# Two attention layers on one core: the transfers that fold the softmax sums, put in another order in two DMA queues

## The chip, the cores and the metric

The kernel runs on one core of a Trainium2 chip. The metric is the device time of one execution in microseconds (us); the median of three runs of the kernel before is 2529.92 us (2529.29 to 2533.68).

The names of a profile are used throughout: PE is the matrix engine (PEld its weight loads), DVE the vector engine, ACT the scalar engine, POOL and SP the two engines that issue the DMA transfers here. POOL's transfers can add to what lies at the destination; SP's only copy.

## The reference

Sixteen images of 256 channels and 32 x 32 positions go through two layers. Each layer normalises its input by groups and adds an attention over the 1024 positions, with 4 heads of 64 channels:

```python
q, k, v = proj(Wq, bq), proj(Wk, bk), proj(Wv, bv)     # of the group-normalised x
sim = jnp.einsum('bhdi,bhdj->bhij', q, k)
qpos = jnp.einsum('hdi,bhdj->bhij', rel, q)            # rel = rel_h + rel_w
attn = jax.nn.softmax(sim + qpos, axis=-1)
out = jnp.einsum('bhdn,bhmn->bhdm', v, attn)
x = x + out                                            # once for each layer
```

All is float32. What matters below is the denominator of the softmax: for every head and position a sum of 1024 exponentials.

## The kernel before, in words

**Units, pairs, blocks.** A unit is one image in one layer (32 of them; images of both layers are interleaved). A unit has two pairs of heads (`pr` 0 and 1), and a pair is worked in two halves of 512 positions. So a unit is four blocks, `n` counts blocks, and `b` is 0 to 3 in a unit. Blocks 0 and 2 of a unit are even ones (the pair's first half), 1 and 3 are odd. `block(n)` writes out by hand, for one block, what every engine is to do and in what order; the program runs in that order on each engine.

**A block's main work.** For each of 8 slices `j`, DVE writes the position term into PSUM (`seed`, L503), PE adds the scores (L539), ACT takes the exponential (L552) into a tile `p`, and PE multiplies the eight `p` with the values (`attend`, L592). ACT moves the result out of PSUM with `take_out` (the COPY of line L653, one for each block). Between these, PE, ACT and DVE do the projections and norms of the next unit.

**The sums.** The eight `p` of a block are added to a denominator in these steps:

- `add_up(blk, 1)`: DVE makes a tile `first` of `p` 0 and 1 (L557), and a POOL transfer adds `p` 2 to it (L568).
- `add_up(blk, 4)` and on: DVE makes a tile `acc` of `p` 3 and 4 (L557) and adds `p` 5, 6 and 7 (L572), the last one in the next block.
- `add_first` (POOL, L609) adds `first` to `acc`: 128 rows.
- `fold` (POOL, L614) adds `acc`'s upper 64 rows to its lower 64.
- `stack_up` (SP, L628, two transfers) copies rows 0 to 31 of each head into a tile `stack`, and `fold_again` (POOL, L633, two transfers) adds rows 32 to 63 there. With that, `acc` has been read for the last time. `stack` holds both halves of a pair.
- `fold_stack` (POOL, L638), five steps, folds the 128 rows of `stack` to 64, 32, 16, 8 and 4; `R` is 32 and `D` is 64, so the steps are `D`, `R`, `R // 2`, `R // 4`, `R // 8`.
- `spread_sums` (SP, L646, four transfers) writes the four rows to `den_all`; DVE takes reciprocals (L688), SP sends them through DRAM (L690, L695), and `finish` (DVE, L703 and L710) normalises and adds the residual. A finished image goes out by L712; the next image comes in by L113.

**Buffers.** `first` and `acc` share a pool of four buffers under one tag, handed out in turn:

```python
apool = ctx.enter_context(tc.tile_pool(name="apool", bufs=4))
```

A block takes two of them, so `acc` of block `n` takes the buffer of `acc` of block `n - 2`, and DVE's L557 waits until both `fold_again` transfers of block `n - 2` have landed. In the same way `first` of block `n` waits for `add_first` of block `n - 2`. There are two `stack` tiles.

**What sets the order.** Each engine works through its own instructions in the program's order. A transfer that waits for another one's landing holds up everything behind it in its queue. In the program before, `fold`, `stack_up` and `fold_again` of an even block stand together in the odd block after it; `stacked` and `summed` are the pairs whose `stack` is folded in odd and even blocks.

Of the kernel before, what the change touches and what calls it, by code (L numbers as in the profile page):

```python
# [56 lines left out]
def fast_path(ctx, tc, sh, x, layers, out, W, den_all, good, flag):  # L57
# [27 lines left out]
    B, C, H, N, CC, NT, NH, D, GT = (  # L85
        sh.B, sh.C, sh.H, sh.N, sh.CC, sh.NT, sh.NH, sh.D, sh.GT
    )
# [86 lines left out]
    def psum2(tag, name):  # L174
        i = 2 * "abcd".index(tag)
        return banks[:, i : i + 2, :]
# [252 lines left out]
    def values(u, g, pv, first=None):  # L429
        l = units[u][1]  # L430
        vts[u, g] = vpool.tile([P, NT // 2, C], F32, tag="v", name=f"v_{u}_{g}")
        pv = pv.rearrange("p a (b c) -> p a b c", c=C)

        def part(t, i, cc, rs, a):
            for x, c in enumerate(QUARTERS):
                j0 = (4 * g + 2 * a + i) * P + x * D
                yield nc.tensor.matmul(  # L437
                    pv[c, a, i, :],
                    xns[u][rs, cc, j0 : j0 + D],
                    W.wv[l][rs, cc, :],  # L440
                    start=(t == 0 and cc == 0 and i == 0),
                    stop=(t == 1 and cc == CC - 1 and i == 1),
                    skip_group_check=True,
                )

        def products(t):
            rounds = [
                [part(t, i, cc, rs, a) for rs, a in BANKS[t]]
                for i in range(2)
                for cc in range(CC)  # L450
            ]
            if t == 0 and first is not None:
                yield from woven(rounds, first)
            else:
                for r in rounds:
                    for p in r:
                        yield from p

        def out_of_psum():
            v = vts[u, g].rearrange("p (a b) c -> p a b c", a=2)  # L460
            for a in range(2):
                nc.scalar.copy(v[:, a], pv[:, a])  # L462

        return stretches(products), out_of_psum
# [62 lines left out]
    def scores(blk, j, tag=None, halves=False):  # L527

        u, pr, half = blk
        ps = psum2(tag, f"ps_{u}_{pr}_{half}_{j}") if tag else seeds.pop((blk, j))  # L530
        columns = slice(half * HALF, (half + 1) * HALF)
        for x, c in enumerate(QUARTERS):
            for h, hs in enumerate(QUARTERS):
                j0 = j * P + x * D
                terms = [(ks[u, pr], qs[u, pr])]
                if tag:
                    terms = [(qs[u, pr], wide[u, pr])] + terms
                for i, (a, b) in enumerate(terms):
                    nc.tensor.matmul(  # L539
                        ps[c, h, :],  # L540
                        a[hs, j0 : j0 + D],
                        b[hs, columns],
                        start=bool(tag) and i == 0,
                        stop=i == len(terms) - 1,
                        skip_group_check=True,
                    )
        p = ppool.tile([P, 2, HALF], F32, tag="p", name=f"p_{u}_{pr}_{half}_{j}")
        if halves:
            for h in range(2):
                nc.scalar.activation(p[:, h, :], ps[:, h, :], AF.Exp, bias=W.shift)  # L550
        else:
            nc.scalar.activation(p, ps, AF.Exp, bias=W.shift)  # L552
        probs[blk, j] = p

    def new_sum(blk, name, a, b):
        t = apool.tile([P, 2, HALF], F32, tag="acc", name=f"{name}_{blk[0]}_{blk[1]}_{blk[2]}")
        nc.vector.tensor_tensor(t, probs[blk, a], probs[blk, b], ALU.add)  # L557
        return t

    def add_up(blk, j):  # L560
        if index[blk] >= FOLDED:
            if j == 1:
                accs[blk] = new_sum(blk, "acc", 0, 1)
            elif j > 1:
                nc.vector.tensor_tensor(accs[blk], accs[blk], probs[blk, j], ALU.add)  # L565
        elif j == 1:
            firsts[blk] = new_sum(blk, "first", 0, 1)
            nc.gpsimd.dma_start(firsts[blk], probs[blk, 2], accum_op=ALU.add)  # L568
        elif j == 4:
            accs[blk] = new_sum(blk, "acc", 3, 4)  # L570
        elif j > 4:
            nc.vector.tensor_tensor(accs[blk], accs[blk], probs[blk, j], ALU.add)  # L572
# [32 lines left out]
    R = P // 4  # L605
    stacks = {}

    def add_first(blk):
        nc.gpsimd.dma_start(accs[blk], firsts.pop(blk), accum_op=ALU.add)  # L609

    def fold(blk):

        acc = accs[blk]
        nc.gpsimd.dma_start(acc[:D], acc[D:], accum_op=ALU.add)  # L614

    def beside(blk):

        u, pr, x = blk
        for h in range(2):
            yield h, stacks[u, pr][2 * x + h : P : 4, :]  # L620

    def stack_up(blk):

        u, pr, x = blk
        if x == 0:
            stacks[u, pr] = spool.tile([P, HALF], F32, tag="stack", name=f"stack_{u}_{pr}")
        for h, at in beside(blk):
            nc.sync.dma_start(at, accs[blk][:R, h, :])  # L628

    def fold_again(blk):  # L630
        acc = accs.pop(blk)
        for h, at in beside(blk):
            nc.gpsimd.dma_start(at, acc[R:D, h, :], accum_op=ALU.add)  # L633

    def fold_stack(u, pr, rows_):

        stack = stacks[u, pr]
        nc.gpsimd.dma_start(stack[:rows_], stack[rows_ : 2 * rows_], accum_op=ALU.add)  # L638

    def spread_sums(u, pr):  # L640

        stack, n = stacks.pop((u, pr)), index[u, pr, 0]
        for x in range(2):
            for h, hs in enumerate(QUARTERS):
                g = 2 * x + h
                nc.sync.dma_start(den_all[hs, n + x, :], stack[g : g + 1, :])  # L646
# [77 lines left out]
    def finish(u, pr):  # L724
        normalise(u, pr)
        add_residual(u, pr)
# [28 lines left out]
    blocks = [(u, pr, half) for u in range(NU) for pr in range(CC) for half in range(NH)]  # L755
# [32 lines left out]
    def block(n):  # L788
# [4 lines left out]
        last = n == len(blocks) - 3  # L793
# [5 lines left out]
        stacked = blocks[n - 3][:2] if not even and n > 2 else None  # L799
        summed = blocks[n - 4][:2] if even and n > 3 else None  # L800
        before = blocks[n - 6][:2] if even and n > 5 else blocks[n - 5][:2] if last else None
        after, previous = blocks[n + 1], blocks[n - 1] if n > 0 else None
        two = u + 2 < NU
        folded = previous and n - 1 < FOLDED
# [5 lines left out]
            add_up(previous, 7)  # L810
        if folded and even:
            add_first(previous)
        if even:
            qk = psum2(tz, f"qk_{w}_{pr}") if not plain else None
            first = None if plain else first_product(w, pr, qk)
            v, v_out = values(w, 1 - b // 2, psum2(tx, f"pv_{w}_{b}"), first)
# [11 lines left out]
                after_first(w, pr, qk)  # L828
            scores(blk, 2)
            add_up(blk, 1)  # L830
            if summed:
                fold_stack(*summed, R // 8)
                spread_sums(*summed)
            v(1)
            if folded:
                fold(previous)
            v_out()
            scores(blk, 3)
            seed(blk, 4, tb)
# [58 lines left out]
            scores(after, 1)  # L898
            seed(after, 2, ta)
            add_up(blk, 6)  # L900
            if summed and n == FOLDED:
                reciprocals(*summed)
            seed(after, 3, tb)
            norms(u, b, 4)
# [3 lines left out]
        else:  # L908
# [8 lines left out]
            if n == 1:  # L917
                reduced(2, 1)
                added(2)
            if stacked:  # L920
                fold_stack(*stacked, D)
            if stacked:
                fold_stack(*stacked, R)
            if not plain:
                k_half(w, pr, 1, qk)
            norms(u, b, 0)
# [11 lines left out]
            norms(u, b, 1)  # L938
            seed(blk, 7, tx)
            add_up(previous, 7)  # L940
            if folded:
                add_first(previous)
            if n > 4 and not last:
# [19 lines left out]
            if two:  # L963
                mean_out = (norm_mean if b == 1 else norm_var)(u + 2, pm)
            scores(after, 0)
            if folded:
                fold(previous)
                stack_up(previous)
            if stacked:
                fold_stack(*stacked, R // 2)  # L970
            if folded:
                fold_again(previous)
            if u + 3 < NU and units[u + 3][1] == 0 and u > 0 or n == 3:
                load_x(units[u + 3][0], range(pr_, pr_ + 1) if u > 0 else range(CC))
            seed(after, 1, tx)
            if last:
                finish(*before)
            if stacked:
                fold_stack(*stacked, R // 4)
                if last:  # L980
                    fold_stack(*stacked, R // 8)
                    spread_sums(*stacked)
            if two:
                mean_out()
                if b == 3:
# [17 lines left out]
    FOLDED = len(blocks) - BPU  # L1003
# [118 lines left out]
    def added(u):  # L1122
        part = parts.pop(u)
        reds[u] = small.tile([P, G], F32, tag="red", name=f"red_{u}")
        nc.vector.tensor_tensor(reds[u], part[:, 0, :], part[:, 1, :], ALU.add)
# [83 lines left out]
    v, v_out = values(0, 0, psum2("d", "pv_0_0"))  # L1209
# [7 lines left out]
    for n in range(len(blocks)):  # L1217
        if n in (1, 2):
            forms(n - 1)
        block(n)  # L1220
# [290 lines left out]
```

## Time and profile before

| what | value |
| --- | --- |
| median of three runs | 2529.92 us |
| the profiled execution | 2537.24 us, of it span 2535.5 us |
| granted clock of PE, mean | 0.995 |
| busy share of the span: PE, DVE, ACT, POOL | 98%, 93%, 81%, 31% |
| transfers from POOL: first<-p, acc<-first, acc<-acc, stack<-acc, median to landing | 8.0, 5.6, 4.5, 2.8 us |
| idle time of POOL before its `stack<-acc` transfers (L633) | 842.2 us |
| idle time of DVE before it makes `acc` (L557) | 32.0 us |

The span is the time from the first to the last instruction of the program in the profiled execution. Busy shares are averages over the span, and matmuls overlap each other, so that a PE of 98% can still lose time in places. A wait is listed with what ended it; "issue" there means that the profile shows nothing that ended it.

### The profile page before, as it was taken

The numbers are of one execution on the slowest core, as the hardware profiler recorded it, in microseconds if no ns is written. First come the engines' busy times: TensorE is split into PE (matmuls) and PEld (weight loads), VectorE is DVE, ScalarE is ACT, GpSimd is POOL, SyncE is SP. The second block draws the span as 40 slices with busy tenths as digits, with TensorE's granted clock in tenths as the row PEclk, the third lists the DMA queues.
The fourth block names the chain that finished last, engine by engine and source line by source line (L and its number), as shares of the span: only waits on it lengthen the run. The fifth ranks groups of instructions, "written<-read, shape, count | busy, mean of one in ns | idle before, by whom it ended". The sixth has DMA issues, their size and how long they took to land. (4 is left out here: it accounts for less than half of the span.)

```text
span 2535.5 us, 86433 instructions
## 1 busy us (share of the span) xinstructions
PE 2482.9 (98%) x36976; PEld 1766.0 (70%) x36976; DVE 2362.9 (93%) x2816; ACT 2057.3 (81%) x4296; POOL 796.4 (31%) x937
## 2 busy tenths in 40 slices
PE   7999999999999999999999999999999999999997
PEld 4777777777767767777676777767776676677764
DVE  7899999999999999899999999999999999899998
ACT  5888888888888888788887888888878888788764
POOL 0223333333333333333332333333333333333230
PEclk9999999999999999999999999999999999999999
DMA  2555556566556555665565556565665555556552
GB/s 86 111 96 104 109 111 112 110 129 137 111 109 141 112 105 111 124 120 113 116 115 118 114 111 121 108 132 115 120 126 119 114 104 112 109 95 122 113 112 73
DMA packets 137704, 286.64 MB, mean 113 GB/s; under 512 B 55896, under 2 KB 57432, under 8 KB 137312
## 3 DMA queue, kind: packets, MB, share of 16 engines
q0 software_dynamic: 71568, 195.12, 44.6%
q1 hardware_dynamic: 65744, 85.90, 11.9%
q8 instruction: 293, 4.80, 0.8%
q14 instruction: 99, 0.81, 0.1%
HBM read 51.78 MB, written 17.30 MB: 27 GB/s over the span
## 5 line engine op out<-in xcount | busy, mean ns | idle before, releaser
L503 DVE TENSOR_TENSOR banks<-abt 128x1024 f32<-128x1024 f32 x1207 | 1239.6, 1060 | 100.5 <-ACT p L552 58.6
L552 ACT ACTIVATE p<-banks,shift 128x1024 f32<-128x1024 f32 x898 | 980.1, 1114 | 278.1 <-PE banks L539 162.4
L539 PE MATMUL banks<-q,k 64*64 64x512 f32 x8192 | 1114.5, 593 | 9.6 <-DVE banks L503 9.6
L592 PE MATMUL banks<-p,v 64*64 64x256 f32 x16384 | 963.6, 377 | 0.0
L592 PEld LDWEIGHTS banks<-p,v 64*64 64x64 f32 x16384 | 783.1, 133 | 182.6 <-issue 38.9
L539 PEld LDWEIGHTS banks<-q,k 64*64 64x64 f32 x8192 | 470.9, 133 | 305.6 <-issue 121.4
L633 POOL DMA_DIRECT2D stack<-acc x248 | 210.8, 964 | 842.2 <-DMA stack<-acc 688.1
L572 DVE TENSOR_TENSOR acc<-acc,p 128x1024 f32<-128x1024 f32 x372 | 454.0, 1220 | 4.2
L638 POOL DMA_DIRECT2D stack<-stack x310 | 309.9, 1000 | 386.4 <-DMA stack<-stack 225.1
L401 PE MATMUL banks<-t,form 64*64 64x512 f32 x1984 | 405.2, 589 | 0.0
L437 PE MATMUL banks<-Wv,xn 64*64 64x256 f32 x4096 | 302.1, 378 | 0.7 <-ACT v L462 0.7
L437 PEld LDWEIGHTS banks<-Wv,xn 64*64 64x64 f32 x4096 | 229.8, 133 | 43.6 <-PEq L193 17.5
L401 PE MATMUL banks<-xn,form 64*64 64x512 f32 x992 | 259.3, 589 | 0.0
L288 ACT ACTIVATE xn<-x,nshift,rstd 128x128 f32<-128x128 f32 x496 | 211.7, 500 | 29.4 <-DVE nshift L281 29.4
L568 POOL DMA_DIRECT2D first<-p x124 | 220.6, 1779 | 36.7 <-ACT p L552 33.3
L614 POOL DMA_DIRECT2D acc<-acc x124 | 103.1, 831 | 386.0 <-DMA acc<-first 373.4
L213 ACT ACTIVATE junk<-x,neg 128x128 f32<-128x128 f32 x505 | 199.9, 404 | 0.0
L609 POOL DMA_DIRECT2D acc<-first x124 | 185.5, 1496 | 36.6 <-DVE acc L572 33.3
L401 PEld LDWEIGHTS banks<-t,form 64*64 64x64 f32 x1984 | 137.7, 133 | 71.1 <-issue 33.9
L557 DVE TENSOR_TENSOR acc<-p,p 128x1024 f32<-128x1024 f32 x128 | 156.2, 1221 | 32.0 <-issue 18.2
L550 ACT ACTIVATE p<-banks,shift 128x512 f32<-128x512 f32 x252 | 159.5, 684 | 23.1 <-PE banks L539 17.3
L557 DVE TENSOR_TENSOR first<-p,p 128x1024 f32<-128x1024 f32 x124 | 150.9, 1217 | 2.4 <-DMA acc<-first 2.1
(102 smaller groups left out, 1761.9 us busy)
## 6 DMA issues: line engine op xcount, KB each, us to landing
first<-p POOLq DMA_DIRECT2D x124, 512.0 KB, 8.0
acc<-first POOLq DMA_DIRECT2D x124, 512.0 KB, 5.6
rden<-rd SPq DMA_DIRECT2D x126, 256.0 KB, 4.4
acc<-acc POOLq DMA_DIRECT2D x124, 256.0 KB, 4.5
x<-in_x_dram SPq DMA_DIRECT2D x32, 512.0 KB, 3.8
stack<-acc SPq DMA_DIRECT2D x248, 64.0 KB, 2.1
stack<-acc POOLq DMA_DIRECT2D x248, 64.0 KB, 2.8
out_dram<-x SPq DMA_DIRECT2D x31, 512.0 KB, 2.9
```

Source lines behind the costliest of these rows:

```text
L288: nc.scalar.activation(grouped(xns[u], g), grouped(xt[units[u][0]], g), AF.Identity, bias=shift[:, g : g + 1], scale=rstd[:, g : g + 1],)
L401: yield nc.tensor.matmul(ps[c, a, :], f[rs, left[a], c0 : c0 + D], right[a][rs, :], start=(t == 0 and step == 1 and a == 1), stop=(t == 1) ...
L437: yield nc.tensor.matmul(pv[c, a, i, :], xns[u][rs, cc, j0 : j0 + D], W.wv[l][rs, cc, :], start=(t == 0 and cc == 0 and i == 0), stop=(t = ...
L503: nc.vector.tensor_tensor(ps[:, h].rearrange("p h (w y) -> p h w y", y=H), ab[:, h, :H].unsqueeze(2).to_broadcast(shape), ab[:, h, H + hal ...
L539: nc.tensor.matmul(ps[c, h, :], a[hs, j0 : j0 + D], b[hs, columns], start=bool(tag) and i == 0, stop=i == len(terms) - 1, skip_group_check ...
L552: nc.scalar.activation(p, ps, AF.Exp, bias=W.shift)
L557: nc.vector.tensor_tensor(t, probs[blk, a], probs[blk, b], ALU.add)
L568: nc.gpsimd.dma_start(firsts[blk], probs[blk, 2], accum_op=ALU.add)
L572: nc.vector.tensor_tensor(accs[blk], accs[blk], probs[blk, j], ALU.add)
L592: yield nc.tensor.matmul(po[c, a, :QUART], vts[u, j // 4][rs, j % 4, c0 : c0 + D], p[rs, h, a * QUART : (a + 1) * QUART], start=(fresh and ...
L633: nc.gpsimd.dma_start(at, acc[R:D, h, :], accum_op=ALU.add)
L638: nc.gpsimd.dma_start(stack[:rows_], stack[rows_ : 2 * rows_], accum_op=ALU.add)
```

## The change

Nothing is added or removed: the same transfers are issued, in another order.

```diff
 even block:
         if folded and even:
             add_first(previous)
+        if summed:
+            fold_stack(*summed, R // 4)
...
             add_up(blk, 1)
+            v(1)
+            if folded:
+                fold(previous)
             if summed:
                 fold_stack(*summed, R // 8)
                 spread_sums(*summed)
-            v(1)
-            if folded:
-                fold(previous)
+            if folded and n > 1:
+                fold_again(blocks[n - 2])
...
 odd block:
             scores(blk, 2, halves=True)
...
-            if stacked:
-                fold_stack(*stacked, D)
-            if stacked:
-                fold_stack(*stacked, R)
...
             add_up(previous, 7)
+            if stacked:
+                fold_stack(*stacked, D)
+                fold_stack(*stacked, R)
             if folded:
                 add_first(previous)
...
             scores(after, 0)
-            if folded:
-                fold(previous)
-                stack_up(previous)
             if stacked:
                 fold_stack(*stacked, R // 2)
             if folded:
-                fold_again(previous)
+                fold(previous)
...
             seed(after, 1, tx)
             if last:
                 finish(*before)
-            if stacked:
+            if last:
                 fold_stack(*stacked, R // 4)
-                if last:
-                    fold_stack(*stacked, R // 8)
-                    spread_sums(*stacked)
+                fold_stack(*stacked, R // 8)
+                spread_sums(*stacked)
+            if folded:
+                stack_up(previous)
```

So an even block's `fold_again` moves from the odd block after it into the next even block, behind that block's `fold`; its `stack_up` moves to the end of the odd block, behind the load of an image; the fourth and third steps of the older pair's stack move as well.

On POOL, in the middle of the program, the rows between two `R` steps (32x512) of the stack before. In a name like acc_4_0_1 the numbers are unit, pair and half, so acc_4_0_0 is an even block's and acc_4_0_1 the odd one's after it; stack_3_1 is the older pair's.

```order
L638 DMA stack_3_1_4061<-stack_3_1_4061 32x512
L609 DMA acc_4_0_0_4320<-first_4_0_0_4171 128x1024
L568 DMA first_4_0_1_4446<-p_4_0_1_2_4392 128x1024
L614 DMA acc_4_0_0_4320<-acc_4_0_0_4320 64x1024
L638 DMA stack_3_1_4061<-stack_3_1_4061 16x512
L633 DMA stack_4_0_4540<-acc_4_0_0_4320 32x512 x2
L638 DMA stack_3_1_4061<-stack_3_1_4061 8x512
L609 DMA acc_4_0_1_4489<-first_4_0_1_4446 128x1024
L568 DMA first_4_1_0_4641<-p_4_1_0_2_4639 128x1024
L638 DMA stack_3_1_4061<-stack_3_1_4061 4x512
L614 DMA acc_4_0_1_4489<-acc_4_0_1_4489 64x1024
L633 DMA stack_4_0_4540<-acc_4_0_1_4489 32x512 x2
```

And the same stretch of POOL's queue in the changed kernel:

```order
L638 DMA stack_3_1_4064<-stack_3_1_4064 32x512
L609 DMA acc_4_0_0_4320<-first_4_0_0_4169 128x1024
L568 DMA first_4_0_1_4446<-p_4_0_1_2_4392 128x1024
L638 DMA stack_3_1_4064<-stack_3_1_4064 16x512
L614 DMA acc_4_0_0_4320<-acc_4_0_0_4320 64x1024
L609 DMA acc_4_0_1_4489<-first_4_0_1_4446 128x1024
L638 DMA stack_3_1_4064<-stack_3_1_4064 8x512
L568 DMA first_4_1_0_4639<-p_4_1_0_2_4637 128x1024
L614 DMA acc_4_0_1_4489<-acc_4_0_1_4489 64x1024
L638 DMA stack_3_1_4064<-stack_3_1_4064 4x512
L633 DMA stack_4_0_4542<-acc_4_0_0_4320 32x512 x2
L633 DMA stack_4_0_4542<-acc_4_0_1_4489 32x512 x2
```

The pair of `fold_again` transfers of the even block stood between that block's `fold` and the odd block's `add_first`; now it stands four transfers later, behind the odd block's `fold`, directly ahead of the odd block's own pair.

On SP, further on, the rows of one odd block and the start of the even block after it, before:

```order
L690 DMA rd_0_16621<-r_16_0_16619 128x16
L695 DMA rden_0_16623<-rd_0_16621 64x1024 x2
L628 DMA stack_0_16727<-acc_0_0_16507 32x512 x2
L113 DMA x_16733<-in_x_dram 128x1024
L646 DMA den_all<-stack_1_16248 64x1x8 x4
L628 DMA stack_0_16727<-acc_0_1_16676 32x512 x2
```

And in the changed kernel:

```order
L690 DMA rd_0_16621<-r_16_0_16619 128x16
L695 DMA rden_0_16623<-rd_0_16621 64x1024 x2
L113 DMA x_16728<-in_x_dram 128x1024
L628 DMA stack_0_16731<-acc_0_0_16507 32x512 x2
L646 DMA den_all<-stack_1_16250 64x1x8 x4
L628 DMA stack_0_16731<-acc_0_1_16676 32x512 x2
```

The load of the image now stands ahead of the even block's `stack_up`; the rest of SP's queue keeps its order.

More of the change, by code (lines that the diff above doesn't have):

```diff
@@ L900, in block @@
             add_up(blk, 6)
-            if summed and n == FOLDED:
+            if n == FOLDED:
                 reciprocals(*summed)
```

## The prediction, made before the changed kernel ran

> **What bounds the kernel now.** I read the page first, then the list of waits, then the order of time on one engine after the other. The page:
>
> ```profile
> span 2535.5 us, 86433 instructions
> PE 2482.9 (98%) x36976; PEld 1766.0 (70%) x36976; DVE 2362.9 (93%) x2816; ACT 2057.3 (81%) x4296; POOL 796.4 (31%) x937
> L633 POOL DMA_DIRECT2D stack<-acc x248 | 210.8, 964 | 842.2 <-DMA stack<-acc 688.1
> ```
>
> PE is the bound, with DVE close behind. POOL is idle for two thirds of the span, but 842.2 us of that it stands before `fold_again` (L633), so its queue may be late although it is not busy. The waits show whom that touches; DVE's only waits for a transfer of any weight are (us in total, times, longest):
>
> ```profile
> DVE acc L557 <- issue: 18.2, 20, 2.7
> DVE acc L557 <- DMA stack<-acc: 13.2, 8, 4.2
> DVE first L557 <- DMA acc<-first: 2.1, 2, 1.2
> ```
>
> Together 33.5 us: DVE wants a new `acc` or `first` and its buffer has not been read yet. Does that reach the end? One case shows it, first DVE's row, then PE's:
>
> ```profile
> 1344.14 1.23 DVE L557 TENSOR_TENSOR acc<-p,p 128x1024 f32<-128x1024 f32 x1 [2.90 <-DMA stack<-acc]
> ...
> 1346.69 0.30 PE L232 MATMUL banks<-sum,avg 64*64 64x16 f32 x8 [2.78 <-DVE banks L225]
> ```
>
> In an odd block DVE's wait of 2.90 us becomes 2.78 us of idle PE at once. The blocks' ends measure all of it, since ACT's COPY of L653 comes once in each block:
>
> ```profile
> 114.17 0.57 ACT L653 COPY od<-banks 128x512 f32<-128x512 f32 x1
> ...
> 497.55 0.57 ACT L653 COPY od<-banks 128x512 f32<-128x512 f32 x1
> 519.17 0.56 ACT L653 COPY od<-banks 128x512 f32<-128x512 f32 x1
> 595.68 0.57 ACT L653 COPY od<-banks 128x512 f32<-128x512 f32 x1
> ...
> 1271.30 0.56 ACT L653 COPY od<-banks 128x512 f32<-128x512 f32 x1
> 1292.93 0.56 ACT L653 COPY od<-banks 128x512 f32<-128x512 f32 x1
> ...
> 2442.14 0.59 ACT L653 COPY od<-banks 128x512 f32<-128x512 f32 x1 [2.33 <-PE banks L592]
> ```
>
> From 519.17 to 595.68 is one unit (four blocks) without such a wait: 76.51 us. From 114.17 to 2442.14 are 120 blocks, 30 units: 2327.97 us. Undisturbed they would take 30 x 76.51 = 2295.30, so 32.67 us are lost, about what DVE waits (33.5). That is the whole of what this change can win in the steady part.
>
> **Why the buffers are late.** POOL's queue over one pair of blocks, with SP's part:
>
> ```profile
> 508.42 1.69 POOL L633 DMA_DIRECT2D stack<-acc  x2 [5.93 <-issue]
> ...
> 510.02 1.87 POOL L609 DMA_DIRECT2D acc<-first  x1
> ...
> 515.90 0.84 POOL L614 DMA_DIRECT2D acc<-acc  x1 [1.97 <-DMA acc<-first]
> 523.86 1.71 POOL L633 DMA_DIRECT2D stack<-acc  x2 [7.11 <-DMA stack<-acc]
> 527.88 0.82 POOL L638 DMA_DIRECT2D stack<-stack  x1 [2.31 <-DMA stack<-acc]
> 530.87 0.78 POOL L638 DMA_DIRECT2D stack<-stack  x1 [2.17 <-DMA stack<-stack]
> 531.39 1.20 POOL L609 DMA_DIRECT2D acc<-first  x1
> ...
> 538.29 0.82 POOL L614 DMA_DIRECT2D acc<-acc  x1 [4.80 <-DMA acc<-first]
> ...
> 544.96 1.69 POOL L633 DMA_DIRECT2D stack<-acc  x2 [5.04 <-DMA stack<-acc]
> ...
> 546.55 1.87 POOL L609 DMA_DIRECT2D acc<-first  x1
> ```
>
> ```profile
> 518.74 2.46 SPq L646 DMA_DIRECT2D den_all<-stack  x4
> 521.30 1.17 SPq L628 DMA_DIRECT2D stack<-acc  x2
> ...
> 541.82 1.67 SPq L628 DMA_DIRECT2D stack<-acc  x2
> ```
>
> The even block's L633 pair starts at 508.42, the next even block's at 544.96: the queue's loop of waits takes 36.54 us, and PE needs 76.51 / 2 = 38.26. With 1.7 us to spare, any slow transfer makes DVE wait. When DVE wants its buffers:
>
> ```profile
> 498.12 2.48 DVE L572 TENSOR_TENSOR acc<-acc,p 128x1024 f32<-128x1024 f32 x2
> 512.84 1.22 DVE L557 TENSOR_TENSOR acc<-p,p 128x1024 f32<-128x1024 f32 x1
> 528.40 1.22 DVE L557 TENSOR_TENSOR acc<-p,p 128x1024 f32<-128x1024 f32 x1
> 534.51 2.48 DVE L572 TENSOR_TENSOR acc<-acc,p 128x1024 f32<-128x1024 f32 x2
> 551.58 1.22 DVE L557 TENSOR_TENSOR acc<-p,p 128x1024 f32<-128x1024 f32 x1
> ...
> 1288.20 1.23 DVE L557 TENSOR_TENSOR acc<-p,p 128x1024 f32<-128x1024 f32 x1 [1.53 <-issue]
> ```
>
> The odd block's `acc` is wanted at 528.40. The odd pair of L633, issued at 523.86, was down before 527.88, where POOL's next transfer had waited for it: half a microsecond in hand, in a block that ran undisturbed.
>
> **The change, part by part.** Durations from issue to landing (min/median/max), for L609, L614 and L633:
>
> ```profile
> L609 POOL DMA_DIRECT2D acc<-first x124: 870/1205/1906, 65.4 to 2455.2; - x124
> DMA to landing us min/median/max: 4.6/5.6/8.0
> L614 POOL DMA_DIRECT2D acc<-acc x124: 815/832/849, 70.3 to 2461.1; - x124
> DMA to landing us min/median/max: 3.4/4.5/6.1
> L633 POOL DMA_DIRECT2D stack<-acc x248: 814/861/1157, 78.1 to 2468.2; - x124
> DMA to landing us min/median/max: 2.5/2.8/5.8
> ```
>
> *The wait taken out of the loop.* Before, from the even block's `fold` (538.29) POOL waited through its landing, SP's copy (541.82), the L633 pair (544.96) and the 8-row stack step until L609 at 546.55: 8.26 us. Now L609 stands right behind that `fold`, one issue later (530.87 to 531.39: 0.52). The loop falls to 36.54 - 8.26 + 0.52 = 28.8 us against 38.26, so POOL no longer paces itself, and L609 starts when DVE's last addition is done.
>
> *The odd block's `acc`.* That addition ended at 498.12 + 2.48 = 500.60, but L609 went at 510.02. Now it goes at about 500.65, 9.4 us earlier, and its `fold` at 506.5 instead of 515.90. SP's spreads wait for the 4-row step, which now stands behind that `fold` and not ahead of it, which costs back some 2 us (landing at about 511.3, 4.8 after the `fold`'s issue; the spreads at 518.74 came 2.84 after it). So the L633 pair goes at about 523.86 - 9.4 + 2 = 516.5 and lands by 520 instead of 527.5, wanted at 528.40. Eight microseconds in hand instead of half a one cover every landing time above. This is where nearly all of the loss lies; I take it as gone. What is late next on this path is nothing of POOL's: DVE then waits for ACT and PE, as it does in undisturbed units.
>
> *The even block's `acc`, the price.* Its L633 pair now follows the odd block's `fold`. Wanted at 512.84: L609 500.65, landed 5.6 later at 506.25, `fold` 0.3 later at 506.55, landed 4.5 later at 511.05; the pair, issued at about 507.6 and 508.2, comes down behind it, 0.85 each as its own issue rows take: 512.75. That is even with the want, and `first<-p`, which stands ahead of the `fold`, may push it; I take 0.7 us late. Between the ends: with the least landings 500.65 + 4.6 + 0.3 + 3.4 + 1.7 = 510.65, 2.2 early; with the longest of each, 516.75, 3.9 late. What does such a wait cost? The even block with DVE's wait of 1.53 us at 1288.20 ended 1292.93 - 1271.30 = 21.63 after the block before it; the undisturbed one took 519.17 - 497.55 = 21.62. So up to 1.5 us costs nothing there, because DVE's next seeds are wanted late. The other even block of a unit has more time: its want, 551.58, is 14.6 us after the addition's end (534.51 + 2.48 = 536.99), against 12.2 here. So one in four blocks is exposed, 30 of them, and pays what goes beyond 1.5 us; with 0.7 us as the middle and landings that scatter by a microsecond I put 0.08 us on each, 2.5 us in all (ends 0 and 30 x (3.9 - 1.5) = 72).
>
> *SP.* The image's load now goes ahead of the even `stack_up`. That copy feeds only the L633 pair which has moved to the next even block, and `fold` before it now goes about 5 us earlier (L609 at its addition rather than 531.39): it has several microseconds, and I cost the load's 0.52 us issue at nothing; if that cover went, the cost would again show in the even `acc`. The stack steps `D` and `R` stand later in the odd block but wait for the same landing, which comes earlier. Their results are wanted a block later. `first` gets its buffer earlier too (the 2.1 us).
>
> *Sum.* The profiled execution took 2537.24 us: its span and 1.7 us around it. 2537.24 - 32.67 + 2.5 = 2507. It is 7.3 us above the median of the runs; undisturbed units repeat within a tenth of a microsecond, so I read those 7.3 us mostly as more waits in that execution, which end at the same floor, and take 2506. If they were the profiler's own, it would be 2499.7.
>
> **A rule against it.** In the stretch above, L609 would go beside DVE's operations on two SBUF tiles (1.22 us each); whether its descriptors suffer, no row separates. The Trainium skill, "SBUF — State Buffer", section "SBUF: two separate sides", says that DVE and GpSimd share a port pair, that a DVE operation with two SBUF inputs holds it for the whole instruction against a GpSimd operation that reads SBUF, and that POOL's descriptors can starve behind DVE. By that rule the sum could be longer by what the third rival gives; landings of 4.6 to 8.0 us, taken while DVE was 93% busy, already hold such delays if there are any, so the trace gives it little weight.
>
> **Rivals.**
>
> 1. *The even `acc` comes too late, and the kernel is slower.* Place: DVE's L557 in the first block of each unit. For: three transfers, one behind the other (L609, the `fold`, the pair), now lie between DVE's addition and its want. Break-even against the median's losses (32.67 - 7.3 = 25.4 us): 25.4 / 30 = 0.85 beyond 1.5, so 2.35 us late each time. At 3 us late: 2506 - 2.5 + 30 x 1.5 = 2549. Against: it needs nearly the longest landings each time.
> 2. *Only part of the odd waits goes*, since transfers of images collide whatever the order: half, 2506 + 12 = 2518. For: the 18.2 us that no semaphore explains. Against: half a microsecond in hand becomes eight.
> 3. *L609 is held by one DVE sum*: the even `acc` comes 1.22 us later, 0.7 + 1.22 = 1.9 late, 0.4 beyond what is free: 30 x 0.4 = 12, so 2518.
> 4. *Nothing changes*, because other waits take the place: 2530. Against: PE's idle time follows DVE's wait one for one.
>
> **How the numbers follow.** The forecast (2499 to 2512): 0.63. Rival 2: 0.10. Rival 3: 0.11. Rival 4: 0.05. Rival 1: 0.11, of which 0.01 lands near the old time and 0.01 below it. A measurement here tells 0.2% (5 us) from no change: under 2524.9 is faster. Faster 0.63 + 0.10 + 0.11 + 0.01 = 0.85, same 0.06, slower 0.09. The range takes the floor by the profiler's reading below and rivals 2 and 3 above: 2499 to 2520.
>
> **What would show it.** Right: DVE's waits before `acc` in odd blocks gone, units of 76.5 us throughout, POOL's 842.2 us before L633 far smaller, L609 starting at the end of DVE's addition. Even blocks may show short waits before `acc` that cost PE nothing. Wrong: waits above 1.5 us before the first block's `acc`, with units longer than 76.5 us all alike.

## The result: 2504.07 us, and the profile after

The changed kernel takes 2504.07 us (median of four runs, 2502.92 to 2504.83). The kernel before, run beside it, takes 2529.63 us (2529.29 to 2533.68). The ratio is 0.9895, 95% interval 0.9878 to 0.9912: 25.6 us less. The profiled execution took 2504.83 us.

The page of the changed kernel, the lines that answer to those of before:

```profile
span 2503.1 us, 86338 instructions
PE 2472.1 (99%) x36976; PEld 1768.8 (71%) x36976; DVE 2360.0 (94%) x2816; ACT 2057.3 (82%) x4296; POOL 790.9 (32%) x937
...
PE 95%; DVE 3%; DMA 0%; issue 0%; ACT 0%; SPq 0%; DVEq 0%; ACTq 0%
...
L633 POOL DMA_DIRECT2D stack<-acc x248 | 239.3, 1176 | 469.6 <-DMA stack<-acc 457.1
...
L557 DVE TENSOR_TENSOR acc<-p,p 128x1024 f32<-128x1024 f32 x128 | 156.0, 1219 | 0.0
L557 DVE TENSOR_TENSOR first<-p,p 128x1024 f32<-128x1024 f32 x124 | 150.9, 1217 | 0.3 <-ACT p L552 0.3
```

The last number of a group is the idle time of its engine ahead of it. Ahead of `acc` (L557) DVE now stands 0.0 us where it stood 32.0, and ahead of `first` 0.3, none of it for a transfer. POOL's 842.2 us ahead of `fold_again` (L633) are 469.6. The third line is the chain that ended last, by engine: PE holds 95% of the span. Before, that chain ran along POOL's and SP's transfers, and could be followed back through a sixth of the span only:

```profile
DMA 8%; issue 3%; DVE 2%; POOL 1%; SPq 1%; PE 1%; ACT 0%; POOLq 0%; DVEq 0%
```

The ends of the blocks, from ACT's order of time (start, duration, instruction):

```profile
113.69 0.56 ACT L653 COPY od<-banks 128x512 f32<-128x512 f32 x1
...
517.85 0.57 ACT L653 COPY od<-banks 128x512 f32<-128x512 f32 x1
594.38 0.57 ACT L653 COPY od<-banks 128x512 f32<-128x512 f32 x1
...
2411.45 0.59 ACT L653 COPY od<-banks 128x512 f32<-128x512 f32 x1 [2.32 <-PE banks L592]
```

The same 120 blocks take 2411.45 - 113.69 = 2297.76 us (2327.97 before), 2.5 above the undisturbed 2295.30; the unit from 517.85 to 594.38 takes 76.53. The span is 2535.5 - 2503.1 = 32.4 us shorter, and 30.2 of that lie here; 0.5 lie ahead of the first of these blocks and 1.7 behind the last one.

POOL's queue and then SP's over the same pair of blocks as in the prediction, which runs 1.3 us earlier here (517.85 against 519.17):

```profile
499.59 0.90 POOL L609 DMA_DIRECT2D acc<-first  x1 [5.87 <-DVE acc L572]
...
506.32 0.82 POOL L614 DMA_DIRECT2D acc<-acc  x1 [3.31 <-DMA acc<-first]
...
507.39 2.33 POOL L633 DMA_DIRECT2D stack<-acc  x2
516.98 0.83 POOL L633 DMA_DIRECT2D stack<-acc  x1 [7.26 <-DMA stack<-acc]
518.57 0.82 POOL L633 DMA_DIRECT2D stack<-acc  x1 [0.75 <-DMA stack<-acc]
521.70 0.83 POOL L638 DMA_DIRECT2D stack<-stack  x1 [2.32 <-DMA stack<-acc]
```

```profile
511.90 2.42 SPq L646 DMA_DIRECT2D den_all<-stack  x4
514.43 1.19 SPq L628 DMA_DIRECT2D stack<-acc  x2
```

The odd block's `add_first` (499.59) now waits 5.87 us for DVE's addition and nothing else: DVE paces the queue, no longer the queue DVE. DVE's side of it:

```profile
496.81 2.48 DVE L572 TENSOR_TENSOR acc<-acc,p 128x1024 f32<-128x1024 f32 x2
...
511.53 1.22 DVE L557 TENSOR_TENSOR acc<-p,p 128x1024 f32<-128x1024 f32 x1
...
525.96 1.21 DVE L557 TENSOR_TENSOR first<-p,p 128x1024 f32<-128x1024 f32 x1
527.09 1.22 DVE L557 TENSOR_TENSOR acc<-p,p 128x1024 f32<-128x1024 f32 x1
```

The addition ends at 499.29, and L609 goes 0.3 us later. The odd pair of L633 is down before 521.70, and `acc` is wanted at 527.09.

**What the order of the buffers had become.** The instructions of the two programs, with what each waits for, show a thing that the prediction had overlooked. DVE's rows in an even block and the odd one after it (the first number in a name is the pair, the second the half; DMAHW are semaphores of SP's transfers, DMASW of POOL's), before:

```
L557 TENSOR_TENSOR acc_0_0_5255<-p_0_0_3_5138,p_0_0_4_5154 128x1024 [waits DMAHW2_49,DMASW7_49,DMAHW3_49,DMASW2_49,DMASW1_49]
L557 TENSOR_TENSOR first_0_1_5381<-p_0_1_0_5242,p_0_1_1_5262 128x1024 [waits DMASW6_49,DMASW4_49]
L557 TENSOR_TENSOR acc_0_1_5424<-p_0_1_3_5337,p_0_1_4_5345 128x1024 [waits DMAHW0_49,DMASW7_49,DMAHW1_49,DMASW1_49,DMASW0_49]
```

And in the changed kernel:

```
L557 TENSOR_TENSOR acc_0_0_5255<-p_0_0_3_5138,p_0_0_4_5154 128x1024 [waits DMASW6_49,DMASW1_49]
L557 TENSOR_TENSOR first_0_1_5381<-p_0_1_0_5242,p_0_1_1_5262 128x1024 [waits DMAHW2_49,DMASW7_49,DMAHW3_49,DMASW6_49,DMASW0_49]
L557 TENSOR_TENSOR acc_0_1_5424<-p_0_1_3_5335,p_0_1_4_5343 128x1024 [waits DMAHW0_49,DMASW4_49,DMAHW1_49,DMASW1_49,DMASW0_49]
```

The semaphores in the traces of the two runs agree. SP's two transfers are `stack_up`, which reads an old `acc`. Before, the even block's `acc` waited for such a buffer. Now it waits for two of POOL's transfers only, those of the `first` of the block before it, and the odd block's `first` gets the old even `acc`, which it wants some 14 us later (525.96 against 511.53). `first` and `acc` share four buffers under one tag; with the even `fold_again` behind `add_first` of the odd block, the buffer of `first` comes free ahead of that of `acc`, and the two swap places. Whether that is worth any time, experiment 3 tells.

### The profile page after: what moved, and what is told of

The parts are those of the page before. It is cut to its first block, busy times and chain, and to the rows that moved or that the text cites. A ratio compares the mean times of both kernels' runs of the same rounds, so it can differ in the third digit from the quotient of the medians.

```text
span 2503.1 us, 86338 instructions
## 1 busy us (share of the span) xinstructions
PE 2472.1 (99%) x36976; PEld 1768.8 (71%) x36976; DVE 2360.0 (94%) x2816; ACT 2057.3 (82%) x4296; POOL 790.9 (32%) x937
## 4 chain that ended last, share of the span: by engine, by line
PE 95%; DVE 3%; DMA 0%; issue 0%; ACT 0%; SPq 0%; DVEq 0%; ACTq 0%
PE banks L539 34%; PE banks L592 34%; PE banks L401 13%; PE banks L437 9%; PE banks L478 2%; PE banks L352 2%; DVE banks L503 1%; DVE acc L565 1%; PE banks L232 0%; DMA den_all<-d 0%; PE banks L309 0%; DVE acc L557 0%; DVE od L703 0%; DVE part L1116 0%; DMA x<-in_x_dram 0%
## 5 line engine op out<-in xcount | busy, mean ns | idle before, releaser
L592 PEld LDWEIGHTS banks<-p,v 64*64 64x64 f32 x16384 | 775.2, 133 | 185.2 <-issue 28.4
L539 PEld LDWEIGHTS banks<-q,k 64*64 64x64 f32 x8192 | 478.4, 133 | 298.6 <-issue 112.4
L633 POOL DMA_DIRECT2D stack<-acc x248 | 239.3, 1176 | 469.6 <-DMA stack<-acc 457.1
L609 POOL DMA_DIRECT2D acc<-first x124 | 113.1, 912 | 424.9 <-DVE acc L572 244.5
L568 POOL DMA_DIRECT2D first<-p x124 | 110.9, 894 | 190.7 <-ACT p L552 113.8
L557 DVE TENSOR_TENSOR acc<-p,p 128x1024 f32<-128x1024 f32 x128 | 156.0, 1219 | 0.0
L557 DVE TENSOR_TENSOR first<-p,p 128x1024 f32<-128x1024 f32 x124 | 150.9, 1217 | 0.3 <-ACT p L552 0.3
```

The lines of the kernel that those rows point to most:

```text
L539: nc.tensor.matmul(ps[c, h, :], a[hs, j0 : j0 + D], b[hs, columns], start=bool(tag) and i == 0, stop=i == len(terms) - 1, skip_group_check ...
L592: yield nc.tensor.matmul(po[c, a, :QUART], vts[u, j // 4][rs, j % 4, c0 : c0 + D], p[rs, h, a * QUART : (a + 1) * QUART], start=(fresh and ...
```

## The experiments

Three accounts could explain the result. By the *loop* theory the gain comes from the move of the even `fold_again` alone: POOL's loop of waits becomes shorter than PE's time. By the *slot* theory it hangs on the swap of the buffers. By the *stack* theory it is the order of the fold steps of the older pair's stack. Each line ahead of a measurement was written before that kernel ran. The kernel before ran beside each group on the same chip and scattered there between 2517 and 2537 us; ratios are against it.

**1. The even `fold_again` alone.** The kernel before, with this edit only:

```diff
             if folded:
                 fold(previous)
+            if folded and n > 1:
+                fold_again(blocks[n - 2])
...
-            if folded:
-                fold_again(previous)
```

> The kernel before, with one part of the change alone: the even block's two fold_again transfers (L633) move into the next even block, behind its fold; every other transfer keeps its place. Loop theory (the gain is the wait taken out of POOL's loop): the queue still meets the older pair's R // 4 step ahead of L609, which waits for R // 2 to land, so of the 8.3 us some 5 remain and the loop is about 33.5 us against 38.26: 2504 to 2510 us, DVE's waits before acc below 5 us in all. Slot theory (the gain is that the even acc is handed another buffer, the one the odd block's first has left): the same hand-over appears here, 2504. Stack theory (the gain is in the older pair's steps that moved): 2520 to 2530.

Measured: 2503.20 us (2502.81 to 2503.45) against 2527.22, ratio 0.9907 (0.9874 to 0.9939). That is the whole gain, so the stack theory, which had put 2520 to 2530 here, falls. The loop and the slot theory had put nearly the same time, and the buffers swap here too: experiment 3 has to tell them apart. From the page of this run, and POOL's order of time in the same stretch:

```profile
L557 DVE TENSOR_TENSOR acc<-p,p 128x1024 f32<-128x1024 f32 x128 | 155.9, 1218 | 0.0
```

```profile
500.21 0.80 POOL L638 DMA_DIRECT2D stack<-stack  x1 [4.80 <-DMA stack<-stack]
500.73 1.22 POOL L609 DMA_DIRECT2D acc<-first  x1
```

Here the 8-row step still stands ahead of `add_first` and holds it to 500.73, and that costs nothing: no wait ahead of `acc`.

**2. The same with the 4-row and 8-row part of the stack's order** (`R // 4` moved into the even block behind its `add_first`, as in the change):

```diff
+        if summed:
+            fold_stack(*summed, R // 4)
...
-            if stacked:
+            if last:
                 fold_stack(*stacked, R // 4)
```

> The kernel before with two parts of the change: fold_again of the even block moved as in the changed kernel, and the older pair's R // 4 step moved behind the even block's add_first. SP's order and the image load stay as before. Loop theory: POOL's loop is then the changed kernel's, about 29 us: 2503 to 2506 us, and no wait of DVE before acc. Slot theory: the same. Stack theory: between 2504 and 2520.

Measured: 2502.33 us (2502.18 to 2503.46), ratio 0.9905 (0.9872 to 0.9937). Within a microsecond of experiment 1: the order of the stack's steps adds nothing.

**3. The changed kernel, with two buffers for `first` and two for `acc`,** so that none can swap:

```diff
-    apool = ctx.enter_context(tc.tile_pool(name="apool", bufs=4))
+    apool = ctx.enter_context(tc.tile_pool(name="apool", bufs=2))
...
-        t = apool.tile([P, 2, HALF], F32, tag="acc", name=...)
+        t = apool.tile([P, 2, HALF], F32, tag=name, name=...)
```

> The changed kernel with two buffers for first and two for acc, kept apart, where both shared four: the even acc then takes the buffer of the even block two before it, as in the kernel before, and waits for that block's fold_again. The order of transfers is the changed one. Loop theory with the price that the prediction put on the even acc (0.7 us late in one block of four, of which 1.5 us are free): DVE waits before acc in the first block of the units, 10 to 40 us in all, and the time is 2504 to 2510 us. Slot theory: the waits of before return, 2525 to 2532.

Measured: 2514.35 us (2510.86 to 2515.24), ratio 0.9950 (0.9931 to 0.9968): some 11 of the 24 us that experiments 1 and 2 gain on this chip are gone, a time between those that the two theories had put. Now DVE does wait ahead of the even `acc` (us in total, times, longest):

```profile
DVE acc L557 <- DMA stack<-acc: 13.7, 8, 8.6
DVE acc L557 <- issue: 8.2, 9, 1.9
```

Sixteen of these are short, 13.3 us together, 0.8 us each on average and the longest 1.9; one takes 8.6 us. ACT's rows tell what they cost, in the steady part and in the block behind it (the block that ends at 2442.34 here ends at 2433.07 in the changed kernel):

```profile
114.09 0.57 ACT L653 COPY od<-banks 128x512 f32<-128x512 f32 x1
...
2411.81 0.58 ACT L653 COPY od<-banks 128x512 f32<-128x512 f32 x1 [2.32 <-PE banks L592]
2442.34 0.58 ACT L653 COPY od<-banks 128x512 f32<-128x512 f32 x1 [1.96 <-PE banks L592]
```

The 120 blocks take 2411.81 - 114.09 = 2297.72 us, as in the changed kernel (2297.76): the short waits cost nothing that can be seen. The block after them takes 30.53 us, against 2433.07 - 2411.45 = 21.62, and the span is 9.6 us longer (2512.7 against 2503.1). That is the one long wait, at the end of the program, where `acc` is made from `p` 0 and 1 (there is no `first` there) and so is wanted early in the block. DVE's row, then POOL's:

```profile
2423.70 1.22 DVE L557 TENSOR_TENSOR acc<-p,p 128x1024 f32<-128x1024 f32 x1 [8.59 <-DMA stack<-acc]
```

```profile
2418.40 0.84 POOL L614 DMA_DIRECT2D acc<-acc  x1 [3.22 <-DMA acc<-first]
2419.05 1.02 POOL L638 DMA_DIRECT2D stack<-stack  x1
2419.67 2.14 POOL L633 DMA_DIRECT2D stack<-acc  x2
```

The even pair of L633 goes at 2419.67, and DVE had wanted the buffer at 2415.1. This wait is not the old order come back, but a price of keeping the buffers apart: here this `acc` can only take the buffer of an older `acc`. In the kernel before, where both share four, the same `acc` took the buffer of a `first`, as what ended its short wait shows:

```profile
2445.80 1.23 DVE L557 TENSOR_TENSOR acc<-p,p 128x1024 f32<-128x1024 f32 x1 [0.37 <-DMA acc<-first]
```

So some 10 of the 11 us are this edit's own, at the program's end. In the steady part the even `acc` waits by the old rule again and nothing is lost by it: the slot theory falls, and the swap is worth nothing that these runs can show.

**4. The changed kernel with the even `fold_again` put back** into the odd block, behind its `stack_up`:

```diff
             if folded:
                 stack_up(previous)
+                fold_again(previous)
...
-            if folded and n > 1:
-                fold_again(blocks[n - 2])
```

> The changed kernel with fold_again of the even block put back into the odd block, behind its stack_up; all else of the change stays. The buffers are handed on as in the kernel before. Loop theory: POOL waits again for fold, copy and landing ahead of the odd block's L609, the loop is back near 37 us of 38.26: 2520 to 2540 us, with DVE's waits before acc in odd blocks back at 20 us or more. Slot theory: 2525 to 2532 as well; it is told from the loop by the run with own buffers. Stack theory: 2504 to 2512.

Measured: 2620.79 us (2615.37 to 2626.06), ratio 1.0371 (1.0332 to 1.0410). The direction was foreseen, the size missed by over 80 us: with the loop closed again, the rest of the change is far worse than the order before, and DVE's waits are back:

```profile
DVE acc L557 <- issue: 46.0, 25, 4.7
DVE acc L557 <- DMA stack<-acc: 38.3, 20, 6.2
```

POOL's rows of two odd pairs of L633, and SP's between them:

```profile
499.59 1.71 POOL L633 DMA_DIRECT2D stack<-acc  x2 [8.11 <-DMA stack<-acc]
...
528.71 0.83 POOL L614 DMA_DIRECT2D acc<-acc  x1 [2.26 <-DMA acc<-first]
...
540.20 1.71 POOL L633 DMA_DIRECT2D stack<-acc  x2 [9.81 <-DMA stack<-acc]
```

```profile
534.38 3.16 SPq L646 DMA_DIRECT2D den_all<-stack  x4
537.65 1.16 SPq L628 DMA_DIRECT2D stack<-acc  x2
```

From pair to pair it is 40.61 us, more than PE's 38.26. Between the odd `fold` at 528.71 and its copy on SP at 537.65 lie 8.94 us; in the kernel before these two stood at 515.90 and 521.30, 5.40 apart. Over the 62 odd blocks the median of that distance, worked out from the trace, is 6.0 us before and 7.7 here. SP's queue holds the copy behind the spreads, and the spreads wait for a stack step that now stands behind the odd `fold`. Two suspects follow: the late spreads, and the image's load ahead of the even copy.

**5. Experiment 4 with the spreads ahead of the odd `fold` again.**

```diff
             add_up(blk, 1)
-            v(1)
-            if folded:
-                fold(previous)
             if summed:
                 fold_stack(*summed, R // 8)
                 spread_sums(*summed)
+            v(1)
+            if folded:
+                fold(previous)
```

> The kernel put back (fold_again of the even block in the odd block again, 2620.79 us), and in addition the older pair's R // 8 step and SP's four spreads stand ahead of the odd block's fold again, as in the kernel before. Open is why putting one pair back cost 93 us more than the kernel before and not the same. Late-spread theory: with fold ahead of R // 8, SP's spreads, and behind them the odd block's copy, come some 2 us later, which lengthens the loop from 36.5 to 38.5 us, beyond PE's 38.26, so that every block waits: here the loop is short again, 2520 to 2545 us. Image-load theory (the copy of the even block stands behind the image load on SP): no change, 2600 to 2625.

Measured: 2541.83 us (2531.60 to 2556.57) against 2527.59, ratio 1.0061 (1.0035 to 1.0087). This is as the late-spread theory had it. It is 79 us less than experiment 4, which lost 94 against the kernel before (the two ran on two chips; their ratios differ by 78 us): 79 / 62 pairs is 1.3 us a pair, and the median distance from the odd `fold` to its copy falls from 7.7 to 5.4 us.

**6. Experiment 4 with the image's load behind the even `stack_up` and `fold_again`.**

```diff
                 fold(previous)
+                stack_up(previous)
+                fold_again(previous)
             if u + 3 < NU and ...:
                 load_x(...)
...
-            if folded:
-                stack_up(previous)
-                fold_again(previous)
```

> The kernel put back (2620.79 us), and in addition the even block's stack_up and fold_again stand ahead of the image load again, as in the kernel before; R // 8 stays behind the odd block's fold. Late-spread theory: little change, 2595 to 2625 us. Image-load theory: 2520 to 2545 us.

Measured: 2596.12 us (2586.13 to 2607.95), ratio 1.0277 (1.0229 to 1.0325): 25 us less than experiment 4, at the lower end of what the late-spread theory had put and far from the image-load theory's 2520 to 2545. With the loop closed, the load's place ahead of the copy costs about 1 us for each of the 26 loads that moved (the other 6 of 32 are issued in the first 17 us). It is the smaller of the two causes. As 79 and 25 are together more than the 94, the two overlap in part.

**7. The changed kernel with the image's load behind the even `stack_up`,** the even `fold_again` where the change has it, **and beside it the changed kernel itself and experiment 2 again,** on one chip.

```diff
                 fold(previous)
+                stack_up(previous)
             if u + 3 < NU and ...:
                 load_x(...)
...
-            if folded:
-                stack_up(previous)
```

> The changed kernel with the even block's stack_up ahead of the image load again. Question: does the order on SP matter once POOL does not wait there? In the changed kernel the load of an image took 9.5 us at the median (3.8 before), and its profiled execution lost 2.7 us in one block where PE stood without a wait that the profile shows. If the load's place matters, 2502 to 2503 us and that loss gone; if not, as the changed kernel, 2503 to 2505.

> The changed kernel again, beside the others on one chip: 2503 to 2505 us. If the loss of 2.7 us in one block belongs to the order, it is there again; if it was chance, the profiled execution is without it.

> The kernel with two parts of the change (fold_again and R // 4 moved; 2502.33 us before) beside the changed one on one chip. If it is really the better of the two, 2502 to 2503 us, 1 to 2 us below the changed kernel; if the difference was that of two chips, the same as the changed one.

Measured: 2502.85 us (ratio 0.9903, 0.9885 to 0.9921), the changed kernel 2502.75 (the same ratio and interval), experiment 2 2502.28 (0.9901, 0.9883 to 0.9919). By its time alone experiment 7 would have read as a gain from the load's place (2502 to 2503 had been put for that); beside the changed kernel on the same chip it is none. Where the copy is wanted a block later, the load's place is worth nothing in the time, and three orders that all hold the moved `fold_again` agree within 0.6 us. None of them beats the changed kernel by more than the runs scatter.

Not tried: a fifth buffer in the kernel before, which might also have taken the wait out, and the swap of the buffers with the loop left closed.

## Why the prediction was right, and where it was not

The measured 2504.07 us lie 1.9 us below the forecast of 2506 and inside the range.

- *32.67 us are all that can be won in the steady part.* Right: 30.2 of them went, and the unit above takes 76.53. That the loss was "about what DVE waits (33.5)" is in part chance. In the trace of the kernel before, 25.5 us of the waits stood in odd blocks, and these lost 31.2; 5.9 us stood ahead of `acc` in even blocks and cost nothing that can be seen. What the odd blocks lost beyond their waits is treated below, under the clock.
- *The wait taken out of the loop carries the change.* Right, and shown by experiments 1 and 3: that move alone gives 2503.2, and the steady part stays without loss where the buffers cannot swap.
- *The odd `acc`: half a microsecond becomes eight.* The terms held, a little short. L609 was put at 500.65, with its own addition; it went 0.3 us behind it. The pair of L633 was put 10.0 us behind the `fold`; it went 10.66 behind (506.32 to 516.98). L609 itself landed later than its median, so that the pair was 17.4 us behind L609 and not 15.9. In that block 5.4 us are in hand (521.70 to 527.09), which is enough. The 2 us put down for the later spreads are right in size: the median distance from odd `fold` to copy grew from 6.0 to 8.0 us.
- *The even `acc`, 2.5 us in all.* This step failed. It took the buffer rule of the kernel before (`acc` takes the buffer of the `acc` two blocks back) for the changed one. There the even `acc` takes the buffer of a `first`, whose transfer was issued at 499.59 and down before 506.32, 5 us ahead of the want at 511.53. The term is 0. Where experiment 3 restores the assumed rule in the steady part, the inner working holds: sixteen waits of 0.8 us on average, where 0.7 was put as the middle, and even the longest, 1.9 us against the 1.5 put down as free, cost nothing visible. So by its own rule too the term would have been 0.
- *The sum* came out right partly by luck. The 2.5 us that the steady part still loses are not the even `acc`'s. They are one stand of PE, 2.7 us in one block, treated below.
- *The 7.3 us of the profiled execution before were waits of that execution.* The runs fit that, though none shows it outright: the changed kernel's profiled execution stands 0.8 us above its median, and the runs of the kernel before scatter over 20 us on other chips, where those of the changed one keep within 3.
- *SP's load costs nothing, under a cover.* Right in the time (experiment 7); what it costs without the cover is in experiment 6.
- *The rule against it* (the Trainium skill, "SBUF — State Buffer", section "SBUF: two separate sides", by which POOL's descriptors can starve behind DVE). The trace shows nothing of it at L609: it follows the addition by 0.3 us at the median, with DVE 94% busy, and its median landing is 5.4 us, against 5.6 before.
- *Rivals.* The first and third needed the even `acc`'s wait, which the swap removed; where experiment 3 has it back it is 0.8 us and not the 2.35 that the first needed, and L609 is not held by a DVE sum, as the third had it. The second (only part goes) fails on the row of 0.0 us ahead of `acc`, the fourth on the time.

## What to carry to other kernels

A queue that is busy a third of the time can still set the pace, if its instructions wait for one another in a ring: add up the waits of one turn and compare them with what the bound engine needs for it. To open such a ring, move the one transfer whose waits close it, and judge every other edit with the ring open and with it closed: the same late spreads and early load cost 79 and 25 us in the one, and nothing in the other. A wait costs by where it stands: up to 1.9 us ahead of an even block's `acc` cost nothing, half a microsecond ahead of an odd one's was lost in full. When readers of shared buffers change places, read anew which buffer the next tile takes; the rule of the old order may not hold. And an edit that is to take one thing out can bring a price of its own, as the separate buffers did at the program's end: look where in the program its time goes.

## What the runs showed that had not been expected

**A load that takes longer where its place costs nothing.** The transfer of an image in, 512 KB, has a median of 3.8 us from issue to landing before and 9.5 in the changed kernel; copies on the same queue became slower too (each first line before, then after):

```profile
x<-in_x_dram SPq DMA_DIRECT2D x32, 512.0 KB, 3.8
rden<-rd SPq DMA_DIRECT2D x126, 256.0 KB, 4.4
```

```profile
x<-in_x_dram SPq DMA_DIRECT2D x32, 512.0 KB, 9.5
rden<-rd SPq DMA_DIRECT2D x126, 256.0 KB, 6.7
```

In experiment 7, with the load behind the copy, it is 6.1, and in experiment 1 it is 5.1. Loads that fall together with POOL's transfers are the likely reason; no run separates it.

**PE stands, and its instructions may have come late.** In the changed kernel's profile one block lost 2.7 us, with these rows of PE and no semaphore that ended the wait:

```profile
920.12 1.02 PE L539 MATMUL banks<-q,k 64*64 64x512 f32 x2
922.82 0.65 PE L539 MATMUL banks<-q,k 64*64 64x512 f32 x3 [1.68 <-issue]
```

In the second profile of the same kernel another block lost 1.7 us and this one nothing; in experiment 3 the same block lost 1.3. The trace has something beside each of the three stands. The page lists a queue named `instruction` (q8) with 293 packets, 16 KB each in the trace. Between 908.64 and 919.94 it moved nothing, while the 16 DMA engines were 95% busy and a load of an image took 11.3 us to land; the next packet was down at 921.40, and PE went on 1.4 us behind it. In the other two executions PE went on 1.6 us behind such a packet. From the start of one packet to the start of the next PE began 505 matmuls and weight loads here, 436 and 464 in the other two; in all the eleven traces no other gap has more than 432, and where both the load stands behind the copy and the loop is open (experiments 1, 2, 7) there is no such stand. So the likely cause is that PE ran out of instructions while the transfers crowded; that is a reading of three cases, and no run separates it.

**The clock after a wait.** Before, a wait of 2.50 us of DVE's left PE idle for 2.37 us until 1033.82, and a wait of 4.21 us of DVE's ended at 2163.45. In the windows around them the mean granted clock (the number ahead of the last two) is 0.91 and 0.86:

```profile
1025.00:1045.00 20.00, 17.63 (x298) 13.40 (x294) 16.36 (x28) 10.90 (x17) 6.75 (x8) 0.91 0.67 139
2155.00:2180.00 25.00, 20.91 (x332) 14.76 (x328) 18.00 (x21) 14.59 (x28) 6.78 (x8) 0.86 0.58 122
```

In the changed kernel, without such waits, the mean over the span is 0.999 against 0.995. By the two lines 0.09 x 20 = 1.8 us and 0.14 x 25 = 3.5 us of full clock are missing there. The two blocks lost 3.98 and 6.72 us by ACT's rows, 1.5 and 2.5 more than DVE's waits, while nearly all other odd blocks with a wait lost only 0.1 to 0.2 us more than it. So some 4 of the 32.67 us may be a slower clock behind the two waits; no run separates it from them.
